# Half-partition loads copied across by ScalarE, and chunk-end rows on GpSimd, in a two-layer convolution

## The chip, the cores and the metric

The kernel runs on one core of a Trainium2 chip. A core has a matrix engine (TensorE), a vector engine (VectorE, DVE in the profile), a scalar engine (ScalarE, ACT), GpSimd (POOL), and a queue engine SP that only issues transfers here. Each engine takes its instructions in the order in which they were written, and an instruction that waits for a semaphore holds up everything behind it on that engine. The metric is the device time of one execution in microseconds (us); less is better.

## What is computed

Two layers of the same form act on a tensor `x` of 8 images, 32 channels and 252 x 252 pixels, in float32. A layer normalises in 16 groups of two channels, convolves with 5 x 5 weights under reflected borders, and adds its input:

```python
def _gn(v, G=16, eps=1e-5):
    g = v.reshape(B_, G, C_ // G, H_, W_)
    m = jnp.mean(g, axis=(2, 3, 4), keepdims=True)
    s = jnp.var(g, axis=(2, 3, 4), keepdims=True)
    return ((g - m) / jnp.sqrt(s + eps)).reshape(v.shape)

x = x + _L0_conv_ref(_gn(x), L0_conv_weight)   # 5x5, padding 2 on each side, mode='reflect'
x = x + _L1_conv_ref(_gn(x), L1_conv_weight)
```

The reference forms the convolution with Fourier transforms. The kernel forms it directly.

## The kernel before, in words

**Layout.** An image is split into its even and odd rows and its even and odd columns. Each of the four combinations of parities, with 32 channels, fills one quadrant of the 128 partitions. The 5 x 5 convolution then is a 3 x 3 one on 126 x 126 points with 128 x 128 weight matrices. In the vertical direction a transform with six points (0 to 5) makes four output rows from six input rows. Normalisation is folded into the weights, which ScalarE scales once per image and layer, and the added input is folded in as `resid`.

**Chunks and slots.** An image has 8 chunks (`NCH`) of 16 rows of such points. A chunk of the first layer (`l = 0`) is read from `x` into a buffer `xs` of 128 partitions by 16 rows by 256 columns. There are two such buffers. A chunk of the second layer (`l = 1`) reads what the first layer left in `y`. The list `order` alternates one chunk of the first layer of image b + 1 and one of the second layer of image b. I call the TensorE work for one chunk a slot.

**A table of times sets the order.** No scheduler moves anything. Each piece of work is entered in a table by `at(t, fn, ...)`; the table is sorted by `t`, and that is the order of the instructions on every engine. The times are only places in that order. `begin(i)` is the place where slot i begins; `t0` and `t1` are the beginnings of the present and the next slot.

**Loading a chunk.** `load` (L143) issues one transfer on SP's queue for each quadrant and run of rows. The partitions 0 to 63 hold the odd columns of the padded row and 64 to 127 the even ones; but every quadrant is loaded with all columns, at an offset of one column. `borders` (L148 to L154) lets GpSimd write the reflected columns, with three small copies for a chunk. Where `once(b, c)` holds, only the two quadrants of partitions 0 to 63 are loaded, and `even_columns` (L159) copies their odd positions to the even positions of partitions 64 to 127. ScalarE does so, except in one case at the start. In the kernel before, `once` holds for chunks 0 to 6 of image 0 and 0 to 2 of image 1.

**The transform of a chunk.** `transform` fills buffers that TensorE reads. VectorE makes differences of rows (`row_pairs`, L562, first layer only), two weighted differences (`row_quads`, L571 and L572, written to the buffer `u12`), the same for the rows that reach into the next chunk (`last_rows`, L578 and L579), and then the six points (L587, L591, L594, L597, L604). For the second layer the sums of rows in `v` come instead from transfers that GpSimd issues (`row_sums`, L552, then the accumulating L554 and L555). `columns` (L613 to L623) prepares points 0 and 5 where they are multiplied "by columns": fewer products, with one step more. Points 0 and 5 then also pass through the tag `u12`, which has one buffer.

**The products.** `conv` has TensorE form points 2 and 4 into `m`, points 1 and 3 into `pairs` (L680), and points 0 and 5 into `sums05` or `extra`. ScalarE seeds `pairs` from `m` (L724, L726), copies `m` (L732) and `pairs` (L739) out, and VectorE combines them (L743 to L766). By columns, `seed_columns` (L706) is a ScalarE instruction between two groups of `extra` products:

```python
        def seed_columns():
            A.activation(middle(2), middle(1), AF.Copy, scale=0.5)
...
            for i in range(4):
                at(t0 + (11.05 if i % 2 else 8.5) + 0.2 * i, column_product, 2 - i % 2, i // 2)
            at(t0 + 9.3, seed_columns)
```

Here `t0` is the slot's beginning; the first group stands at 8.5, the seed at 9.3, the second group, which adds onto the seeded sums, at 11.05. `reflect` (L864 to L867) writes the borders of `y`, `store` copies results to `o` (L917), `squares` (L855) and `piece_sums` (L231, L237) collect statistics, all on ScalarE.

## Time and profile before

| | us |
|---|---|
| Median of three runs | 1892.61 |
| Lowest and highest | 1891.02, 1893.24 |
| The profiled execution's own time | 1893.14 |
| Its span in the profile | 1891.4 |
| TensorE (PE) busy | 1851.5 |
| VectorE (DVE) busy | 1698.0 |
| ScalarE (ACT) busy | 1401.1 |
| GpSimd (POOL) busy | 372.9 |

The span runs from the first to the last recorded instruction, and the profiled execution's time is a little longer. A busy time is the time in which an engine had an instruction under way. Waits are told apart by what ended them: "PE extra L702 <- ACT extra L706" is time in which TensorE stood before the instruction of line 702 until ScalarE's instruction of line 706 was done. Lines of the order of time give start, duration, engine, source line, operation, output and input; a bracket tells how long the engine had been idle before, and what ended that.

### The profile page before, as it was taken

How to read it: one execution, taken by the hardware profiler on the slowest of the kernel's cores; microseconds unless marked ns; L12 is line 12 of the kernel's file. 1: busy time of each engine (PE TensorE's matmuls, PEld its weight loads, DVE VectorE, ACT ScalarE, POOL GpSimd, SP SyncE). 2: the span in 40 equal slices, each digit the busy share in tenths (PEclk: the TensorE clock that was granted, in tenths of full speed). 3: DMA queues.
4: the chain of work that ended last, by engine and by line, in shares of the span. 5: the costliest groups of instructions: out<-in, count | busy, mean ns of one | idle time of the engine just before them, and what ended most of it. 6: DMA issues, size and time to landing. Idle time of an engine off the chain costs nothing.

```text
span 1891.4 us, 20043 instructions
## 1 busy us (share of the span) xinstructions
PE 1851.5 (98%) x5162; PEld 956.7 (51%) x5162; DVE 1698.0 (90%) x2972; ACT 1401.1 (74%) x2695; POOL 372.9 (20%) x733
## 2 busy tenths in 40 slices
PE   5999999999999999999999999999999999999997
PEld 4444455545555555544555455555555545554455
DVE  7987899999998999999899898999989999998685
ACT  5887678778777787778787687877787765565665
POOL 4543211120112210131111310113111131111210
PEclk8999999999999999999999999999999999999999
DMA  9887899999999999999999989999999978995785
GB/s 278 205 176 191 201 248 230 212 229 253 219 239 239 206 249 233 212 244 219 246 224 229 220 214 258 221 227 226 215 260 220 236 184 177 193 203 145 192 217 113
DMA packets 248627, 411.41 MB, mean 218 GB/s; under 512 B 19520, under 2 KB 215488, under 8 KB 238144
## 3 DMA queue, kind: packets, MB, share of 16 engines
q1 hardware_dynamic: 220384, 272.09, 61.8%
q0 software_dynamic: 27648, 135.28, 28.7%
q10 hardware_dynamic: 480, 2.77, 0.4%
q8 instruction: 41, 0.67, 0.2%
q14 instruction: 74, 0.61, 0.1%
HBM read 207.41 MB, written 67.39 MB: 145 GB/s over the span
## 4 chain that ended last, share of the span: by engine, by line
PE 76%; DVE 9%; DMA 8%; ACT 3%; issue 2%; POOL 1%; SPq 0%; DVEq 0%; ACTq 0%; POOLq 0%
PE m L680 27%; PE pairs L680 26%; PE sums L680 8%; PE sums L702 6%; PE extra L702 6%; DMA v<-y 4%; PE extra L680 4%; DMA st<-in_x_dram 1%; DMA xs<-in_x_dram 1%; DMA out_dram<-o 1%; DVE sd L743 1%; ACT o L917 1%; DMA v<-ytail 1%; DVE t L604 1%; POOL u L479 0%
## 5 line engine op out<-in xcount | busy, mean ns | idle before, releaser
L680 PE MATMUL pairs<-t,u 128*128 128x504 f32 (+2 forms) x1548 | 690.4, 585 | 2.7 <-ACT pairs L726 1.6
L680 PE MATMUL m<-t,u 128*128 128x508 f32 (+3 forms) x1560 | 675.2, 581 | 7.1 <-DVE t L591 2.6
L680 PEld LDWEIGHTS m<-t,u 128*128 128x128 f32 x1560 | 293.3, 189 | 325.6 <-issue 297.4
L680 PEld LDWEIGHTS pairs<-t,u 128*128 128x128 f32 x1548 | 289.2, 189 | 321.5 <-issue 295.6
L917 ACT COPY o<-y 64x508 f32<-64x508 f32 x496 | 327.2, 660 | 8.9 <-DMA out_dram<-o 0.2
L743 DVE SCALAR_TENSOR_TENSOR sd<-sd,pairs 128x504 f32<-128x504 f32 (+2 forms) x258 | 163.9, 670 | 19.2 <-PE pairs L680 16.0
L680 PE MATMUL sums<-t,u 128*128 128x508 f32 (+5 forms) x408 | 175.3, 578 | 0.0
L855 ACT ACTIVATE junk<-y,negk 128x1008 bf16<-128x1008 f32 (+1 forms) x144 | 147.4, 1024 | 30.6 <-PE extra L702 14.9
L726 ACT COPY pairs<-m 128x504 f32<-128x504 f32 (+1 forms) x129 | 72.5, 562 | 129.6 <-PE m L680 110.0
L732 ACT COPY sd<-m 128x504 f32<-128x504 f32 (+2 forms) x258 | 137.0, 583 | 32.0 <-DVE sums L789 24.7
L604 DVE SCALAR_TENSOR_TENSOR t<-v 128x1024 f32<-128x1024 f32 (+1 forms) x128 | 157.5, 1230 | 3.5 <-PE sums L680 3.5
L702 PE MATMUL extra<-sdiff,wc 128*128 128x252 f32 (+3 forms) x616 | 156.3, 375 | 3.3 <-ACT extra L706 2.6
L702 PEld LDWEIGHTS extra<-sdiff,wc 128*128 128x128 f32 x616 | 113.5, 188 | 89.6 <-issue 50.2
L591 DVE SCALAR_TENSOR_TENSOR t<-v 128x512 f32<-128x512 f32 (+2 forms) x129 | 89.7, 695 | 65.6 <-DMA v<-y 47.7
L702 PE MATMUL sums<-d,u 128*128 128x252 f32 (+3 forms) x616 | 142.3, 373 | 0.0
L562 DVE TENSOR_TENSOR v<-xs 128x1792 f32<-128x1792 f32 (+1 forms) x65 | 129.5, 1993 | 1.8 <-issue 0.7
L554 POOL DMA_DIRECT2D v<-y x64 | 55.2, 863 | 377.7 <-DMA v<-y 377.7
L702 PEld LDWEIGHTS sums<-d,u 128*128 128x128 f32 x616 | 115.3, 189 | 26.9 <-issue 11.8
L237 ACT ACTIVATE st<-st,negk 128x1134 f32<-128x1134 f32 x98 | 121.7, 1242 | 3.2
L148 POOL COPY xs<-xs 64x32 f32<-64x32 f32 (+3 forms) x74 | 34.1, 461 | 450.2 <-DMA xs<-in_x_dram 330.7
L680 PEld LDWEIGHTS sums<-t,u 128*128 128x128 f32 x408 | 75.9, 188 | 80.1 <-issue 77.2
L231 ACT ACTIVATE st<-st 128x1134 f32<-128x1134 f32 x98 | 112.2, 1145 | 4.0 <-DMA st<-in_x_dram 2.8
(171 smaller groups left out, 2424.7 us busy)
## 6 DMA issues: line engine op xcount, KB each, us to landing
xs<-in_x_dram SPq DMA_DIRECT2D x176, 504.0 KB, 12.6
v<-y POOLq DMA_DIRECT2D x64, 1032.0 KB, 5.7
st<-in_x_dram SPq DMA_DIRECT2D x111, 567.0 KB, 6.9
out_dram<-o SPq DMA_DIRECT2D x488, 126.0 KB, 5.7
v<-y POOLq DMA_DIRECT2D x64, 903.0 KB, 9.9
u<-ud SPq DMA_DIRECT2D x15, 1152.0 KB, 5.6
xs<-in_x_dram SPq DMA_DIRECT2D x30, 441.0 KB, 6.7
xs<-in_x_dram SPq DMA_DIRECT2D x28, 472.5 KB, 11.1
```

The lines of the kernel that those rows point to most:

```text
L231: A.activation(junk, src, AF.Identity, accum_out=acc[:, 0, i : i + 1])
L237: A.activation(junk, src, AF.Square, bias=negk, accum_out=acc[:, 1, i : i + 1])
L562: V.tensor_sub(v[:, r0:r1], t[:, r0 + 2 : r1 + 2], t[:, r0:r1])
L591: stt(ts[b, l, c][0][:, 1, j0:j1], vt[:, :, 1], -2.0, vt[:, :, 2], ALU.mult, ALU.add)
L604: stt(t, got["vt"][:, :, 0:2], 4.0 if l else -4.0, got["vt"][:, :, 2:4], ALU.mult, ALU.add)
L680: T.matmul(dst, u[:, k, 2 - i, :], rhs[:, j0 + i0 : j0 + i1, i : i + wo], start=(i == 0 and not add), stop=(i == 2), skip_group_check=add,)
L702: T.matmul(dst[:, 0, use], w, rhs[:, use], start=(i == 2), stop=True, skip_group_check=(i != 2))
L726: A.copy(dst, src)
L732: A.copy(got["sd"][:, 1 + e], m24[e][:, 0:n])
L743: stt(d, d, -2.0, pairs13[e][:, 0:n], ALU.mult, ALU.add)
L855: A.activation(dst, src, AF.Square, bias=negk, scale=1.0 if i else -1.0, accum_out=acc[:, 1, at_ : at_ + 1])
L917: copy(got["o", h][halves[s], 0:m, cp::2], got["y"][halves[cp], r : r + m, :])
```

## The change

Three things change. First, `once` now holds for all chunks but the last of every image, except for chunk 2 of images 2 to 7. This makes 40 more chunks that load two quadrants and are copied across by ScalarE. They are loaded in one part, and load, borders and copy have new places in the order: load at 7.5 where it stood at 9.5, borders at 5.1 of the next slot where they stood at 9.0, the copy at 6.3. Second, `last_rows` runs on GpSimd, but for the first layer of image 0; the weighted difference, one instruction on VectorE, is two on GpSimd. Third, `last_rows` stands earlier, at 2.1 instead of 3.2 after the start of the transform, for the second layer and for the first layer from image 2 on.

```diff
     def once(b: int, c: int) -> bool:

-        return c < (NCH - 1, 3)[b] if b < 2 else False
+        return c < NCH - 1 and (b < 2 or c != 2)

     def parts(b: int, c: int):

         if once(b, c):
+            if b > 1 or (b == 1 and c > 2):
+                return ((0, ROWS),)
             return ((0, 10), (10, 6)) if (b, c) == (0, 0) else ((0, 2), (2, 14))
...
             u2, (t, nxt) = got["u"][:, 1], source()
+            eng = V if b + l == 0 else G
+            f = 4.0 if l else -4.0
+            if eng is V:
+                stt(u2[:, NT - 1], t[:, ROWS - 2], f, nxt[:, 0], ALU.mult, ALU.add)
+            else:
+                G.tensor_scalar(u2[:, NT - 1], t[:, ROWS - 2], f, None, ALU.mult)
+                G.tensor_add(u2[:, NT - 1], u2[:, NT - 1], nxt[:, 0])
             if l == 0:
-                V.tensor_sub(got["v"][:, ROWS - 2 : ROWS], nxt[:, 0:2], t[:, ROWS - 2 : ROWS])
-            stt(u2[:, NT - 1], t[:, ROWS - 2], 4.0 if l else -4.0, nxt[:, 0], ALU.mult, ALU.add)
+                eng.tensor_sub(got["v"][:, ROWS - 2 : ROWS], nxt[:, 0:2], t[:, ROWS - 2 : ROWS])
...
-            for dt, fn in ((2, row_quads), (3.2, last_rows), (3.6, point2)):
+            for dt, fn in ((2, row_quads), (3.2 if l == 0 and b < 2 else 2.1, last_rows), (3.6, point2)):
...
                 for part in parts(*inputs[k]):
-                    early = once(*inputs[k]) or nb == 0
-                    at(t0 + (14.0 if nb == 0 and part[0] == ROWS else 4.0 if early else 9.5), load, *inputs[k], *part)
-                    at(t1 + (0.2 if early else 9.0), borders, *inputs[k], *part)
-                    if once(*inputs[k]):
-                        kb, kc = inputs[k]
-                        t = 5.25 if part[0] == 0 and (kb, kc) != (1, 0) else 13.55 if kb else 8.5
-                        at(t1 + t, even_columns, *inputs[k], *part)
+                    kb, kc = inputs[k]
+                    if kb > 1 or (kb == 1 and kc > 2):
+                        at(t0 + (7.5 if once(kb, kc) else 9.5), load, kb, kc, *part)
+                        at(t1 + (5.1 if once(kb, kc) else 9.0), borders, kb, kc, *part)
+                        if once(kb, kc):
+                            at(t1 + 6.3, even_columns, kb, kc, *part)
+                    else:
...
```

In the branch left out at the end the lines of before stand unchanged.

## The prediction

> **What bounds the kernel now.** I read the page's totals first, then TensorE's waits, then one slot of the order of time on three engines. A slot is the work of one chunk on TensorE; first-layer (l = 0) and second-layer (l = 1) slots alternate.

> ```profile
> PE 1851.5 (98%) x5162; PEld 956.7 (51%) x5162; DVE 1698.0 (90%) x2972; ACT 1401.1 (74%) x2695; POOL 372.9 (20%) x733
> ...
> PE   5999999999999999999999999999999999999997
> ...
> DMA  9887899999999999999999989999999978995785
> ```

> TensorE is full from the second slice to the last, and the transfers nearly are. That busy share counts pipelined matmuls, so I read the waits too:

> ```profile
> PE m L999 <- DMA st<-in_x_dram: 15.1, 1, 15.1
> PE m L680 <- DVE t L591: 2.6, 2, 2.0
> PE extra L702 <- ACT extra L706: 2.6, 9, 0.9
> PE m L680 <- DVE var L369: 2.1, 1, 2.1
> ```

> The 15.1 us lie in the head, which the change leaves alone. All other waits that the list gives TensorE come to about 15 us, of which some 12 lie behind the head. So nothing taken from another engine can win more than some 10 us (0.5%), while a new wait ahead of a matmul costs its full length.

> One slot of l = 0 near 250 us, TensorE, then ScalarE, then VectorE (start, duration, engine, line):

> ```profile
> 252.64 3.54 PE L680 MATMUL pairs<-t,u 128*128 128x504 f32 x8
> 256.02 1.01 PE L702 MATMUL extra<-sdiff,wc 128*128 128x252 f32 x4
> 256.87 1.85 PE L680 MATMUL pairs<-t,u 128*128 128x504 f32 x4
> 258.56 1.01 PE L702 MATMUL extra<-sdiff,wc 128*128 128x252 f32 x4
> ```

> ```profile
> 253.31 1.07 ACT L732 COPY sd<-m 128x504 f32<-128x504 f32 x2
> 255.43 0.58 ACT L739 COPY sd<-pairs 128x504 f32<-128x504 f32 x1 [1.04 <-PE pairs L680]
> 255.90 0.23 ACT L864 COPY y<-y 128x16 f32<-128x16 f32 x1
> ...
> 257.07 0.57 ACT L706 ACTIVATE extra<-extra 128x504 f32<-128x504 f32 x1 [0.36 <-PE extra L702]
> ```

> ```profile
> 253.46 1.21 DVE L617 TENSOR_TENSOR d<-t 128x1008 f32<-128x1008 f32 x1
> 254.70 0.70 DVE L571 SCALAR_TENSOR_TENSOR u<-y 128x516 f32<-128x516 f32 x1
> ```

> The second group of `extra` products (258.56) needs ScalarE's seed at L706, which ends at 257.64: 0.92 us to spare. L617, the last step of `columns`, ends 3.9 us ahead of that group. Over the slots of this kind it ends between 1.6 and 3.9 us ahead; 3.9 is where VectorE has caught up with TensorE (in the even-chunk slots perhaps 0.5 more).

> [...] the copy of 64x14 elements that takes 0.20 us alone took 2.01 us at 71.59, beside VectorE's L562 (71.50 to 73.53), and near our slot a copy of 64x32, 0.23 us alone, took 1.25 us beside L617:

> ```profile
> 253.52 1.25 POOL L148 COPY xs<-xs 64x32 f32<-64x32 f32 x1 [6.70 <-DMA xs<-in_x_dram]
> ```

> [...] Here the clock stood at half after the 15.1 us wait; the 2.1 us waits left it at full.

> **The change, part by part.**

> 1. VectorE loses `last_rows` in 56 chunks of l = 0 (L578 and L579, 0.72 us from start to next start) and 64 of l = 1 (0.43): 40 + 28 = 68 us of 1698. TensorE hides VectorE's work almost wholly, so this is worth nothing by itself.

> 2. GpSimd gets 56 x 3 + 64 x 2 = 296 instructions. No row has 128-element forms. Between L479 (64 elements, 457 ns) and L459 (384 elements, about 1255 ns) lie 2.5 ns an element: an estimate of 0.6 us for 128 and 0.9 for 256. VectorE pays part of it back in blocked time (L591 took 1.50 us instead of 0.69 at 90.86, beside a 384-element L459): bounds 0 and 56 x 2.1 + 64 x 1.2 = 194 us. I take half, so VectorE's total hardly falls. What hides it is VectorE's slack of about 10%.

> 3. Forty chunks load two quadrants instead of four: 98 issues less on SP's queue, 41 MB less of 411. Before, four quadrants took about 17.7 us from first issue to the last landing and the first two 8 to 13; now two must land. The reload still waits for the last reader of its buffer, formerly L579, now GpSimd's. Gain on the path: at most the few waits that a transfer caused, near 190 us and in isolated slots. I count -4 us.

> 4. ScalarE gets 40 copies of 64x2048. L159 took 1.85 us for 1792 and 0.43 for 256, so 2.1 us each, 84 us in all. ScalarE has room for the sum (74%), but where they stand matters. In the order of the built program each stands behind the two L732 copies and ahead of L739, the four reflections (L864 to L867) and the seed L706. In 33 of the 40 the slot is one by columns, with a seed that TensorE waits for; the other 7 are in a last-chunk slot.

> 5. What the copy waits for is the heart of it. It needs `borders` (three GpSimd copies); these stand on GpSimd behind `last_rows` of the second layer; and that must wait until L617 has read the buffer in which it writes (the tag u12, one buffer). Before, ScalarE's seed depended on no GpSimd instruction, and `borders` had nobody in a hurry behind it.

> So, from the end of L617 (time 0): GpSimd's scale is blocked by L571 (0.7), takes 0.6, the add is held up by L572 and ends near 2.1; three border copies take 0.55 alone and up to 1.6 when L587 and L597 come between. I take 3.2 us; bounds 1.9 (nothing blocked) and 3.7. Hand-over to ScalarE about 0.1; copy 2.1; L739 to the end of L706 1.8 (255.43 to 257.64, less the 0.36 wait there); hand-over to TensorE 0.1. Sum 7.3 us after L617, where TensorE's second group comes 3.9 after it. It stalls 3.4 us. Behind it on TensorE's queue stand the `sums` products and the whole next slot. Where VectorE is later than 3.9 the first stall is longer, but each stall lets VectorE catch up, so 3.9 is the lasting value. It does not improve by itself: L617 hangs on the previous slot's pair products, which TensorE finishes later too.

> Sum: 33 x 3.4 = 112; seven last-chunk slots, where the copy pushes L739 and the root at L371 by about 2 us but VectorE has 2 to 4 us of room before the next products, 1 us each (bounds 0 and 3), 7; freed transfers -4. Together +115. The profiled execution had a span of 1891.4 and a time of 1893.1, near the median of 1892.6; I add to that median and round down a little, because at even chunks the freed 0.7 us of VectorE can widen the 3.9: 2004.

> **The rivals.**

> [...] If GpSimd's five instructions run in 1.9 us and the spare is 3.9 to 4.4, the stall is 1.6 to 2.1 us: 33 x 1.6 to 2.1 is 53 to 69, with the last-chunk slots 1946 to 1970. For it: some GpSimd copies in the trace run unstretched beside VectorE. Against: two stretched examples above.

> *A worse stall.* If GpSimd needs 3.7 and the landing of two quadrants (12 us after a late issue) or VectorE's lag adds another 1 us[...], each slot loses 4.5 or more: 33 x 4.5 = 149 and some 10 around it, 2050 and up.

> *Not slower: the chain is hidden.* With 68 us less on VectorE and a tenth less traffic, the waits of VectorE on the row sums (L591 on the transfer to v, 47.7 us) may vanish and VectorE run further ahead. The point from which it decides: L617 would have to end over 7.3 us ahead of the second `extra` group (6.0 if nothing is blocked) instead of 3.9. Then only the gain of part 3 is left: 1883 to 1893. Against it: in the slots where VectorE waits for nothing but TensorE, the distance is 3.8 to 3.9 again and again. That the change doesn't do what it says I exclude: in the built program VectorE has 176 instructions less, GpSimd 296 and ScalarE 40 more.

> **How the numbers follow.** The chain with a blocked GpSimd (stall 2.5 to 4 us, 1972 to 2040): 0.66. [...] Worse: 0.11. Hidden: 0.10, of which faster 0.05, same 0.03, slower 0.02. A difference of 0.2% (3.8 us) is about what a measurement of this kernel can tell from none. The range leaves out the hidden case and most of the worse one: 1946 to 2048. Slower is 0.66 + 0.13 + 0.11 + 0.02 = 0.92.

> **What would show it.** TensorE's waits would have a line for L702 on ScalarE's seed (L714 in the new numbering) near 110 us in 33 to 40 waits of about 3.4 us, instead of 2.6 us in 9. ScalarE's timeline would show the 64x2048 copy idle ahead of `borders` for 2 to 3 us. GpSimd's 128-element instructions would take over 0.6 us beside VectorE. VectorE's waits on the transfer to v would shrink, and the DMA row fall by about a tenth. I am wrong if the copy runs right behind L732 without waiting, if `extra` waits under 1 us, or if TensorE's wait appears elsewhere, at `m` or `pairs`.

## The result, and the profile after

The changed kernel took 2082.2 us (median of four runs, 2080.2 to 2086.0), beside 1892.6 for the kernel before on the same chip: a ratio of 1.1006, 95% interval 1.0987 to 1.1025. The forecast was 2004 with a range of 1946 to 2048. The direction was right; the loss of 190 us was well above the 112 forecast, and outside the range.

In the changed file the lines of `row_quads` and of what stands above it in the transform are 2 further down, and those behind `last_rows` are 8 further down: L571 is now L573, L591 is L599, L617 is L625, L680 is L688, L702 is L710, L706 is L714, L739 is L747. `last_rows` itself is at L584, L585 and L587.

The page of the changed kernel: busy time of each engine, then TensorE's and the transfers' rows in forty slices.

```profile
PE 1912.7 (92%) x5162; PEld 986.3 (47%) x5162; DVE 1706.0 (82%) x2796; ACT 1477.0 (71%) x2735; POOL 654.0 (31%) x1029
...
PE   6998989989899898998899988999889998999997
...
DMA  9768669677587675776667856777667765465785
```

TensorE runs the same 5162 instructions, now with holes in every second or third slice, and it is *busier* by 61.2 us. The span grew by 188.3 us, from 1891.4 to 2079.7: 61.2 are busy time, and 127.1 are TensorE's idle time (167.0 instead of 39.9). The transfers' row fell, with 370.13 MB moved instead of 411.41.

The waits of the changed kernel (engine, line and what it waited for, then us in total, times, longest):

```profile
POOL u L584 <- DVE d L625: 425.1, 47, 18.4
...
ACT xs L159 <- POOL xs L151: 147.4, 43, 4.8
...
PE extra L710 <- ACT extra L714: 127.5, 41, 5.9
...
DVE t L595 <- POOL u L585: 21.6, 47, 2.5
...
DVE t L599 <- DMA v<-y: 7.3, 3, 4.4
```

From the top this is the forecast chain: GpSimd's `last_rows` (L584) waits for `columns` (L625), ScalarE's copy (L159) for `borders` (L151), TensorE for the seed (L714). TensorE's wait was 2.6 us in all before and is 127.5 now, about what its idle time grew by. VectorE's wait on the transfer to `v` fell from 47.7 to 7.3.

One slot of l = 0 near 265 us, in order of time (start, duration, engine, line). VectorE ends `columns` and goes on to the next transform:

```profile
262.80 1.21 DVE L625 TENSOR_TENSOR d<-t 128x1008 f32<-128x1008 f32 x1
264.04 0.70 DVE L573 SCALAR_TENSOR_TENSOR u<-y 128x516 f32<-128x516 f32 x1
```

GpSimd can begin only then, with `last_rows` and then `borders`:

```profile
264.17 0.97 POOL L584 TENSOR_SCALAR u<-y 128x129 f32<-128x129 f32 x1 [8.30 <-DVE d L625]
265.22 0.41 POOL L585 TENSOR_TENSOR u<-u,y 128x129 f32<-128x129 f32 x1
265.58 0.23 POOL L148 COPY xs<-xs 64x32 f32<-64x32 f32 x1
265.75 0.67 POOL L150 COPY xs<-xs 64x16 f32<-64x16 f32 x1
266.37 0.73 POOL L151 COPY xs<-xs 64x16 f32<-64x16 f32 x1
```

ScalarE stands idle for 3.34 us, copies, and comes to the seed last:

```profile
267.12 2.02 ACT L159 COPY xs<-xs 64x2048 f32<-64x2048 f32 x1 [3.34 <-POOL xs L151]
269.17 0.58 ACT L747 COPY sd<-pairs 128x504 f32<-128x504 f32 x1
...
270.35 0.57 ACT L714 ACTIVATE extra<-extra 128x504 f32<-128x504 f32 x1
```

Here one sees that ScalarE takes its instructions in order: the input of L747 is ready near 264.8 (an estimate: 2.8 us after the pair products begin, as in the slot shown of the kernel before), yet L747 starts only at 269.17, behind the copy.

TensorE, for its second `extra` group:

```profile
266.27 1.85 PE L688 MATMUL pairs<-t,u 128*128 128x504 f32 x4
270.97 1.12 PE L710 MATMUL extra<-sdiff,wc 128*128 128x252 f32 x4 [2.85 <-ACT extra L714]
```

From the end of L625 (264.01): `last_rows` is done 1.6 us later, `borders` 3.1, the copy 5.1, the seed 6.9. The forecast had 2.1, 3.2, 5.4 and 7.2. Its two hand-overs of 0.1 us were 0.02 to ScalarE (267.10 to 267.12) and 0.05 to TensorE (270.92 to 270.97). TensorE's second group was due 4.1 us after L625 (forecast 3.9) and stood for 2.85.

The first by-columns slot of an image's copies is worse, and here the added busy time shows itself. TensorE near 460 us:

```profile
451.48 1.12 PE L710 MATMUL extra<-sdiff,wc 128*128 128x252 f32 x4
...
460.13 2.05 PE L710 MATMUL extra<-sdiff,wc 128*128 128x252 f32 x4 [5.84 <-ACT extra L714]
461.97 6.08 PE L688 MATMUL sums<-t,u 128*128 128x508 f32 x12
```

The group behind the stall takes 2.05 us where the like group before it took 1.12, and the twelve `sums` products 6.08 where the kernel before needed 5.27 for twelve. TensorE's clock is at half after the stall: the granted clock is 0.50 from 456.75 to 463.57 us, and was 1.00 from 447.8 to 452.0. In the records of the granted clock, half-clock stretches last 24.2 us in all before (head and end only) and 143.9 after, in 25 stretches.

How much of the 61.2 us is that? Only the time in which TensorE works at half clock costs anything, and in part of these stretches it stands idle. At half clock a product of 128x508 starts every 847 ns (median of 31 in the changed kernel), at full clock every 426. Laid over each other, the records of the clock and of the products give 107.4 us of busy time at half clock, and 5.4 before. At twice the time for a product, half of the added 102.0 is lost: 51.0 us (an estimate from these two records). The other 10.2 I put down to the breaks themselves. TensorE's records, whose ends are modelled, form 31 unbroken pieces before and 70 after, and each break costs near 0.27 us of busy time: without a wait the group took 1.01 us and its record overlapped that of the group ahead by 0.16 (258.56, where the one ahead ends at 258.72); behind a wait at full clock it takes 1.12 and overlaps nothing.

### The profile page after: what moved, and what is told of

Its sections match the earlier page's. It is cut to its first block, busy times and chain, and to the rows that moved or that the text cites. A ratio compares the mean times of both kernels' runs of the same rounds, so it can differ in the third digit from the quotient of the medians.

```text
span 2079.7 us, 20123 instructions
## 1 busy us (share of the span) xinstructions
PE 1912.7 (92%) x5162; PEld 986.3 (47%) x5162; DVE 1706.0 (82%) x2796; ACT 1477.0 (71%) x2735; POOL 654.0 (31%) x1029
## 2 busy tenths in 40 slices
DMA packets 206100, 370.13 MB, mean 178 GB/s; under 512 B 17952, under 2 KB 172960, under 8 KB 195616
## 5 line engine op out<-in xcount | busy, mean ns | idle before, releaser
L688 PE MATMUL pairs<-t,u 128*128 128x504 f32 (+2 forms) x1548 | 692.2, 586 | 6.1 <-ACT pairs L732 3.8
L688 PE MATMUL m<-t,u 128*128 128x508 f32 (+3 forms) x1560 | 680.6, 585 | 4.1 <-DVE var L371 2.1
L688 PEld LDWEIGHTS m<-t,u 128*128 128x128 f32 x1560 | 297.8, 192 | 324.9 <-issue 299.9
L688 PEld LDWEIGHTS pairs<-t,u 128*128 128x128 f32 x1548 | 290.3, 189 | 326.4 <-issue 299.3
L710 PE MATMUL extra<-sdiff,wc 128*128 128x252 f32 (+3 forms) x616 | 177.6, 414 | 129.5 <-ACT extra L714 127.5
L710 PEld LDWEIGHTS extra<-sdiff,wc 128*128 128x128 f32 x616 | 119.9, 205 | 231.6 <-ACT extra L714 173.0
L159 ACT COPY xs<-xs 64x2048 f32<-64x2048 f32 (+4 forms) x59 | 101.0, 1715 | 147.8 <-POOL xs L151 147.4
L584 POOL TENSOR_SCALAR u<-y 128x129 f32<-128x129 f32 x64 | 56.2, 879 | 431.3 <-DVE d L625 406.8
L688 PE MATMUL sums<-t,u 128*128 128x508 f32 (+5 forms) x408 | 185.7, 606 | 0.0
L554 POOL DMA_DIRECT2D v<-y x64 | 39.7, 620 | 403.6 <-DVE t L612 377.9
L710 PE MATMUL sums<-d,u 128*128 128x252 f32 (+3 forms) x616 | 158.3, 404 | 0.0
L710 PEld LDWEIGHTS sums<-d,u 128*128 128x128 f32 x616 | 127.2, 208 | 31.9 <-issue 10.6
L595 DVE TENSOR_TENSOR t<-u 128x512 f32<-128x512 f32 (+2 forms) x129 | 100.4, 778 | 35.3 <-POOL u L585 21.6
L584 POOL TENSOR_SCALAR u<-xs 128x128 f32<-128x128 f32 x56 | 65.3, 1166 | 193.3 <-ACT pairs L734 107.7
```

The lines of the kernel that those rows point to most:

```text
L159: copy(t[64:128, :, 0:256:2], t[0:64, :, 1:256:2])
L584: G.tensor_scalar(u2[:, NT - 1], t[:, ROWS - 2], f, None, ALU.mult)
L595: V.tensor_sub(ts[b, l, c][0][:, 0, j0:j1], got["u"][:, 1, j0:j1], got["u"][:, 0, j0:j1])
L688: T.matmul(dst, u[:, k, 2 - i, :], rhs[:, j0 + i0 : j0 + i1, i : i + wo], start=(i == 0 and not add), stop=(i == 2), skip_group_check=add,)
L710: T.matmul(dst[:, 0, use], w, rhs[:, use], start=(i == 2), stop=True, skip_group_check=(i != 2))
```

## The experiments

Ten kernels were run. Each edit is against the changed kernel, unless the text says otherwise.

**The copy behind the seed.** Only the place of the copy moves.

```diff
-                            at(t1 + 6.3, even_columns, kb, kc, *part)
+                            at(t1 + 9.4, even_columns, kb, kc, *part)
```

> The changed kernel with one number changed: the copy by ScalarE stands at 9.4 of the slot, behind the seed of the extra products, instead of at 6.3 ahead of it. Theory A (the loss is the chain columns, last_rows, borders, copy, seed, with the copy in front of the seed, plus the halved clock behind it): the waits of TensorE for the seed fall from 127.5 us to under 10, no clock loss in the middle, 1885 to 1900 us. Theory B (GpSimd's instructions slow VectorE[...], and TensorE then waits for VectorE): hardly a change, above 2040. Theory C (ScalarE has no room for 40 copies of 2 us wherever they stand): still above 1940, with waits for pairs or seeds elsewhere.

Measured: 1944.0 us, ratio 1.026 [1.0242, 1.0279]. TensorE's waits in this kernel:

```profile
PE pairs L688 <- ACT pairs L732: 34.8, 21, 3.2
...
PE extra L710 <- ACT extra L714: 2.2, 11, 0.2
```

The wait for the seed of L714 is gone, and 138 of the 190 us with it. But the copy still waits for `borders` (59.4 us in 37 waits), and now the next seed behind it, L732 of the pair products, is late. The expected 1885 to 1900 missed that.

**`borders` ahead of `last_rows` on GpSimd.** They stood at 5.1, just behind; now just ahead.

```diff
-                        at(t1 + (5.1 if once(kb, kc) else 9.0), borders, kb, kc, *part)
+                        at(t1 + (4.9 if once(kb, kc) else 9.0), borders, kb, kc, *part)
```

> The changed kernel with borders at 4.9 instead of 5.1, so that on GpSimd the three border copies stand ahead of the second layer's last_rows and no longer behind its wait for columns. The copy stays ahead of the seed. Theory A: the copy starts when ScalarE is free or the two quadrants have landed, so the stall falls from 3.2 us and more to between 0 and 1.5 us a slot and the clock stays up: 1895 to 1945 us. Theory B: as the changed kernel, above 2040. Theory C: above 1940.

Measured: 1998.8 us, ratio 1.0571 [1.0543, 1.06]. The waits of this kernel:

```profile
POOL xs L148 <- DMA xs<-in_x_dram: 413.7, 52, 14.6
...
PE extra L710 <- ACT extra L714: 71.1, 36, 4.4
...
DVE t L595 <- POOL u L585: 67.3, 52, 3.1
```

Freed from `last_rows`, the first border copy waits for the two quadrants to land, and `last_rows`, now behind it, is late for VectorE. So `borders` were held by two things that end near one another, and taking one away wins 83 us, not the 137 to 187 expected.

**`last_rows` back on VectorE.**

```diff
-            eng = V if b + l == 0 else G
+            eng = V
```

> The changed kernel with last_rows back on VectorE; half loads, borders and the copy ahead of the seed stay. Theory A: on GpSimd borders now wait only for the two quadrants to land, as in the run with borders first (1999 us), so the copy is still held up, by the transfer instead of by columns: 1975 to 2010 us, TensorE's waits for the seed 50 to 80 us. Theory B (GpSimd's rows slow VectorE[...]): clearly less, below 1940. A third reading, that the wait on columns was all that held up the copy: 1893 to 1925.

Measured: 1958.3 us, ratio 1.0331 [1.0303, 1.036], below the range of the first expectation (1975 to 2010) and above the two others. The waits of this kernel:

```profile
POOL xs L148 <- DMA xs<-in_x_dram: 469.1, 58, 23.5
...
ACT xs L159 <- POOL xs L151: 65.5, 36, 4.9
...
PE extra L710 <- ACT extra L714: 44.5, 28, 3.5
```

Without GpSimd in the chain the landing holds `borders` again, and TensorE still waits 44.5 us. Both legs, `last_rows` and the landing, are real; either alone costs tens of us while the copy stands ahead of the seed.

**`last_rows` on GpSimd alone.** The kernel before, with this part and its earlier place only; loads, borders and copies are as before.

```diff
+            eng = V if b + l == 0 else G
...
+                G.tensor_scalar(u2[:, NT - 1], t[:, ROWS - 2], f, None, ALU.mult)
+                G.tensor_add(u2[:, NT - 1], u2[:, NT - 1], nxt[:, 0])
...
+                eng.tensor_sub(got["v"][:, ROWS - 2 : ROWS], nxt[:, 0:2], t[:, ROWS - 2 : ROWS])
...
-            for dt, fn in ((2, row_quads), (3.2, last_rows), (3.6, point2)):
+            for dt, fn in ((2, row_quads), (3.2 if l == 0 and b < 2 else 2.1, last_rows), (3.6, point2)):
```

> The kernel before with last_rows on GpSimd and its earlier place alone; loads, borders and copies as before, so no copy by ScalarE after image 1, chunk 2. Theory A: within 10 us of before, 1888 to 1903, since nobody in a hurry stands behind GpSimd's wait. Theory B: most of the loss is here, above 2000. Theory C: as before, 1893.

Measured: 1900.1 us (20 runs, 1893.8 to 1909.3), ratio 1.0042 [1.0032, 1.0051]. The totals of its page:

```profile
PE 1852.5 (98%) x5162; PEld 956.3 (51%) x5162; DVE 1702.2 (90%) x2796; ACT 1401.0 (74%) x2695; POOL 644.9 (34%) x1029
```

VectorE has 176 instructions less, and its busy time rose from 1698.0 to 1702.2: what it saved it paid in longer instructions, in a kernel in which GpSimd has 272 us more of recorded work. No run takes apart why they are longer. TensorE is unmoved, so this part costs almost nothing without the copy behind it. The 8 us of the median aren't seen in the profiled execution, which took 1893.8, the lowest of the twenty; their cause stays open.

**The copy at the slot's end.** Only the place of the copy moves, behind all that the slot has for ScalarE.

```diff
-                            at(t1 + 6.3, even_columns, kb, kc, *part)
+                            at(begin(i + 2) - 0.05, even_columns, kb, kc, *part)
```

> The changed kernel with the copy moved to the end of the slot, behind the seed, the statistics and the squares, right ahead of the outer rows of the second layer (L776), where ScalarE waits for TensorE. Theory A (only the place of the copy on ScalarE's queue costs time): TensorE waits for nothing new, no clock loss, 1885 to 1903 us. Theory C (ScalarE has no room for 40 copies of 2 us): seeds of pairs are late as in the run with the copy behind the seed (1944 us), above 1925.

Measured: 1912.4 us, ratio 1.0096 [1.0081, 1.0112]. The waits of this kernel on ScalarE's seeds:

```profile
PE pairs L688 <- ACT pairs L732: 8.5, 20, 2.9
...
PE extra L710 <- ACT extra L714: 1.8, 8, 0.2
```

So 170 of the 190 us hang on the place of the copy. Everything else of the change is still in this kernel: GpSimd's `last_rows`, the halved loads, the 40 copies.

**The same, and `last_rows` on VectorE.** Both edits together.

```diff
-            eng = V if b + l == 0 else G
+            eng = V
...
-                            at(t1 + 6.3, even_columns, kb, kc, *part)
+                            at(begin(i + 2) - 0.05, even_columns, kb, kc, *part)
```

> The copy at the end of the slot as before, and last_rows back on VectorE: the half loads alone, with a copy nobody waits for. last_rows on GpSimd alone cost 8 us (1900 against 1892), so Theory A expects 5 to 10 us less than with the copy last and the rows on GpSimd, 1882 to 1895; if freeing VectorE helps once transfers are fewer, it is the other way round.

Measured: 1904.1 us, ratio 1.0056 [1.0041, 1.0071]: 8.3 less than the kernel with the copy at the slot's end, inside the expected step of 5 to 10, though the level was missed by 9. What remains, 11.5 us (10.7 beside runs of the kernel before on the same chip), is 40 copies on ScalarE and half the loads. TensorE waits 8.3 us for L732, of which 2.9 in one place and some 0.28 each in the others: the copy stands just ahead of that seed.

**The copy behind that seed too.** `last_rows` on VectorE, the copy 2.75 after the start of the next slot.

```diff
-            eng = V if b + l == 0 else G
+            eng = V
...
-                            at(t1 + 6.3, even_columns, kb, kc, *part)
+                            at(begin(i + 2) + 2.75, even_columns, kb, kc, *part)
```

> The kernel with the copy at the slot's end and the rows on VectorE still took about 12 us more than the kernel before, and TensorE waited 8.3 us for the pair seed of line 732, which stands just behind the copy. This kernel moves the copy behind that seed (2.75 after the start of the next slot). If the pair seed carries the rest, its line falls to about the 1 to 2 us of the kernel before and the time is 1893 to 1898. If the rest is ScalarE's greater load wherever the copy stands, 1901 to 1906. If the copy is now too late for VectorE's rows of the next chunk, a new wait of VectorE on ScalarE's copy appears and the time is above 1908.

Measured: 1919.1 us, ratio 1.0135 [1.0114, 1.0156]. The waits of this kernel on ScalarE's seeds:

```profile
PE extra L710 <- ACT extra L714: 18.5, 21, 1.3
...
PE pairs L688 <- ACT pairs L732: 2.3, 3, 1.0
```

The pair seed is on time, as expected, and the time is above 1908, but not for the reason given: VectorE waits under 2 us for the copy. The seed of L714 in the second layer's slot is late instead, up to 1.3 us. None of the four places tried makes the copy of 2 us free. No version run beats the kernel before.

**Filling the wait.** Does the halved clock cost what the records say? Fourteen products of an identity, which change no result, keep TensorE at work ahead of the waiting group in the 33 slots.

```diff
...
+        def keep_busy():
+            T.matmul(m24[1][:, 0:P], ident, ident, start=True, stop=True)
...
             at(t0 + 9.3, seed_columns)
+            if copied(b, l, c):
+                for _ in range(14):
+                    at(t0 + 11.04, keep_busy)
```

> The changed kernel, and in the 33 slots where the copy stands ahead of the seed TensorE gets 14 small products of the identity, 128 columns each, about 3 us in all, into a bank that is free there, right before the group that waits for the seed. The wait for the seed stays, only filled. If the 60 us of the loss that the wait itself does not cover are the clock[...]: the clock stays up and the time falls by 45 to 65 us to between 2017 and 2037. If the low clock has another cause[...], filling the waits leaves it at 2075 or above.

Measured: 2045.5 us, ratio 1.0807 [1.0791, 1.0823]: adding 108 us of useless work (33 groups of 3.29) made the kernel 37 us *faster*. Half-clock stretches fell from 143.9 to 38.0 us, and TensorE's busy time in them from 107.4 to 19.8, which gives back 43.8. The expected 2017 to 2037 was missed, mainly because the filling and what is left of the wait come to 139.3 us (108.4 + 30.9) where the wait alone was 127.5. From the span after, 2079.7 + 11.8 - 43.8 makes 2047.7; the profile has 2042.6, and these 5 us have no place in the sum.

**Half of the copy moved.** If the clock drops for long stalls only, stalls shorter by 1 us should leave it alone. Eight rows stay at 6.3, eight go to the slot's end; line numbers are 4 higher.

```diff
+    def half_copy(b: int, c: int, h: int):
+        r = slice(8 * h, 8 * h + 8)
+        A.copy(xs[b, c][64:128, r, 0:256:2], xs[b, c][0:64, r, 1:256:2])
...
-                            at(t1 + 6.3, even_columns, kb, kc, *part)
+                            at(t1 + 6.3, half_copy, kb, kc, 0)
+                            at(begin(i + 2) - 0.05, half_copy, kb, kc, 1)
```

> Of each of the 40 copies only the first 8 rows stay ahead of the seed; the other 8 are copied at the slot's end. Each stall ahead of the second extra group should be 1.0 us shorter: 127.5 becomes about 95. [...] Then the stalls of 2.85 to 3.85 us, now 1.8 to 2.9, leave it at full, and only the first slot of each image (5.84, now 4.8) still lowers it: half-clock stretches of 50 to 75 us in all instead of 144, TensorE busy 1868 to 1880, and the time 2005 to 2020. Rival: the clock follows TensorE's mean idle share and not the single stall. Then it loses in proportion, about 45 us instead of 61: half-clock stretches of 105 to 120 us, busy about 1897, and the time 2030 to 2045.

Measured: 2052.7 us, ratio 1.0844 [1.0822, 1.0865]. Both expectations fell. The wait shrank as it should, to 95.5 us, but half-clock stretches *rose*, to 154.9 us in 34 stretches, and TensorE's busy time to 1917.8. The stall of one and the same slot can be compared in the two kernels. TensorE's order of time in the changed kernel:

```profile
495.95 1.12 PE L710 MATMUL extra<-sdiff,wc 128*128 128x252 f32 x4 [3.25 <-ACT extra L714]
```

In this kernel:

```profile
489.82 2.05 PE L714 MATMUL extra<-sdiff,wc 128*128 128x252 f32 x4 [2.36 <-ACT extra L718]
```

After 3.25 us idle the group runs at full speed, after 2.36 at half. The length of the stall does not decide.

What does decide is in the clock records of all kernels. In the twelve profiles (before, after and these ten) every change of the clock falls on a grid of 3.413 us. I laid that grid over TensorE's busy and idle times, with one shift of 11.2 us between the clock's records and the span for all of them. The shift was chosen so that it fits, but the traces bear it out: in their own timestamps the spans begin at 10.9 to 11.3 us, and with each trace's own value the five counts are 0 of 6378, 13 of 37, 78 of 78, 0 of 91 and 22 of 22. A shift that is off by 0.3 us fits less well (72 of 79 in the third line). The head and the end are left out.

| clock in a cell of 3.41 us | TensorE idle in that cell | next cell at half clock |
|---|---|---|
| full | under 1.7 us | 0 of 6369 |
| full | 1.7 to 2.05 us | 15 of 36 |
| full | over 2.05 us | 76 of 76 |
| half | under 0.5 us | 0 of 91 |
| half | over 0.64 us | 22 of 22 |

The 3.25 us of the first line lie across two cells, 1.61 and 1.64 us in each; the 2.36 us of the second lie with 2.20 in one cell. (The last kernel, below, is counted in the table; without it the rule reads the same.)

**Splitting the wait.** The test of that reading, on the kernel with the half copies: four products, which change no result, that can start when ScalarE's copy of L747 is done, so that they cut the wait in two.

```diff
...
+        def split_wait():
+            T.matmul(m24[1][:, 0:P], ident, got["sd"][:, 0, 0:P], start=True, stop=True)
...
+            if copied(b, l, c):
+                for _ in range(4):
+                    at(t0 + 11.04, split_wait)
```

> The kernel with the half copies, and four products of 128 columns (about 0.9 us) that TensorE can start as soon as ScalarE's copy of line 747 is done, some 1.2 us before the awaited seed; they change no result. A wait of 2.4 us becomes about 1.2 idle, 0.9 busy, 0.3 idle, and ends no earlier. Reading of the clock records so far: the clock is set anew every 3.41 us, and goes to half where TensorE was idle for more than about 1.9 us of the 3.41 before. If that holds, only the first slot of each image (4.96, now some 3.7 in one piece) still halves it: half-clock stretches of 40 to 65 us in all instead of 155, TensorE's busy time falls from 1918 to 1892 to 1902 although it has 30 us more work, and the time falls from 2052.7 to 1998 to 2014. If the halving hangs on the length of the wait or on what the other engines do, the stretches stay near 155 us, busy rises to about 1948 and the time stays at 2045 to 2058.

Measured: 2030.1 us, ratio 1.073 [1.071, 1.075]. TensorE in the slot of the line shown above (L721 is the added product):

```profile
483.58 1.16 PE L721 MATMUL m<-sd,ident 128*128 128x128 f32 x8 [1.19 <-ACT sd L758]
484.76 1.12 PE L718 MATMUL extra<-sdiff,wc 128*128 128x252 f32 x4
```

The group runs at full speed again. Half-clock stretches fell from 154.9 us to 58.3, from 34 to 12, inside the expected 40 to 65: the halving hangs on idle time within a cell. The time was missed by 16 us, and TensorE's busy time, 1919.8, by 18. The four products take 1.16 us at full clock (38.2 in all, not 30), and the clock gives back 40.5 (busy time at half clock 38.3 instead of 119.3): 1917.8 + 38.2 - 40.5 makes 1915.5, and some 4 us have no place in this sum.

| kernel | us | span of the profile | TensorE idle | TensorE busy | half-clock stretches | busy at half clock |
|---|---|---|---|---|---|---|
| before | 1892.6 | 1891.4 | 39.9 | 1851.5 | 24.2 | 5.4 |
| after | 2082.2 | 2079.7 | 167.0 | 1912.7 | 143.9 | 107.4 |
| half of the copy at the slot's end | 2052.7 | 2051.8 | 134.0 | 1917.8 | 154.9 | 119.3 |
| `borders` first | 1998.8 | 1995.9 | 111.3 | 1884.6 | 69.6 | 47.0 |
| `last_rows` on VectorE | 1958.3 | 1953.8 | 82.9 | 1870.9 | 48.7 | 28.3 |
| copy behind the seed | 1944.0 | 1943.3 | 78.0 | 1865.3 | 38.7 | 19.1 |
| copy at the slot's end | 1912.4 | 1909.2 | 51.4 | 1857.8 | 28.9 | 8.4 |
| the same, rows on VectorE | 1904.1 | 1900.5 | 46.9 | 1853.6 | 21.4 | 3.6 |

Down this path the 189.6 us are 169.8 for the place of the copy (after to copy at the slot's end), 8.3 for `last_rows` on GpSimd, and 11.5 for the rest. The parts don't add in any order: with the copy left in its place, `last_rows` on VectorE alone gives back 123.9.

## Why the prediction was right and wrong

**What bounds the kernel: right.** TensorE had nothing to win. With the copy out of the way and `last_rows` on VectorE, 41 MB less traffic left the kernel 11.5 us slower than before, not faster, though it still carried the 40 copies; with `last_rows` on GpSimd, VectorE's lighter program wasn't lighter in time either. That its total "hardly falls" was right: it rose by 4.2 us in the kernel that changed this alone.

**Parts 4 and 5, the chain: right, link by link.** The slot shown has 1.6, 3.1, 5.1 and 6.9 us where the sum had 2.1, 3.2, 5.4 and 7.2. The lines named in advance appeared: the wait at L710 for the seed (127.5 us in 41 waits, 32 of them over 2 us, forecast near 110 in 33 to 40), the copy idle ahead of `borders`, the shorter wait on `v`. The moved copy shows that the chain is the cause, and not only the place where time is booked: 170 us go with it alone. Two smaller things were otherwise. In the slot shown only the scaling in `last_rows` took over the 0.6 us named (0.97; the add took 0.41); and the landing of the two quadrants, which the text put under the worse stall, is a second leg close behind the first: with `last_rows` back on VectorE, TensorE still waits 44.5 us for the seed.

**The lasting spare of 3.9 us: wrong in one slot of each of six images.** "Each stall lets VectorE catch up, so 3.9 is the lasting value" holds in most slots, whose stalls are 2.85, 3.25 and 3.85 us. In an image's first by-columns slot with a copy, the chain was 7.5 us long (L625 ended at 452.54, the seed at 460.07), 0.6 more than in the slot shown, and L625 ended only 1.7 us ahead of the due time, 454.28, so that the stall was 5.84. Six images pay this anew. It makes the mean stall 3.75 instead of 3.4: 120 us in 32 stalls where the sum had 112.

**The sum: it lacked a term of 61 us.** This is the step that failed. Each stall was priced at its own length, with TensorE's clock left at full. As measured, the 188.3 us of the span are 127.1 of idle time, where the sum had 115, and 61.2 of added busy time, where it had nothing: 51.0 for work at half clock and 10.2 for the breaks. The profile before has the clock at half in its head and at its end alone: it stood at half after the wait of 15.1 us and at full after those of 2.1, and nothing in it lies between the two. So what a stall of 3.4 us does to the clock was not shown, and leaving it at full was an estimate. The clock records of the twelve profiles show it: cells of 3.413 us on a grid that doesn't follow the stalls, and about 2 us of idle time inside one cell were enough (over 2.05 us in 76 of 76 cells). A stall of 3.4 us leaves at least 1.7 us in one of two neighbouring cells and up to all of it, so by these records most such stalls halve the clock. In the changed kernel, 20 of the 32 stalls over 2 us at L710 did. The added products and the split wait show that this term is real.

**The last-chunk slots: half the size.** 7 us were counted, 1 us for each of seven slots. The stalls came one slot later, at the seed of the second layer. The first of them, and the same place in the kernel before:

```profile
416.01 1.03 PE L710 MATMUL extra<-sdiff,wc 128*128 128x256 f32 x4 [0.74 <-ACT extra L714]
```

```profile
392.36 1.02 PE L702 MATMUL extra<-sdiff,wc 128*128 128x256 f32 x4 [0.21 <-ACT extra L706]
```

There are six, of 0.74 to 1.05 us, 5.5 us in all, beside 2.0 in the same six places before: 3.5 more. With the copy at the slot's end no wait for this seed is longer than 0.2 us, so they hang on the copy's place too. One new wait of 3.2 us, for the pair seed near 197 us, was not forecast.

**Rivals.** The rival with a stall of 1.6 to 2.1 us asked for GpSimd's five instructions in 1.9 us; they took 3.1 in the slot shown. "Hidden" asked for L625 to end 7.3 us ahead; it ended 4.1 ahead where it was earliest among the slots read closely. The rival that came true is the worse stall (2050 and up), and mostly not by a longer chain: the 3.7 us that it asked of GpSimd were 3.1 in the slot shown and the mean stall was 3.75 us, while 51.0 us are work at half clock. How much GpSimd's instructions lose to VectorE's beside them in this chain (the scaling took 0.97 us beside L573, the add 0.41) no run takes apart.

**My own expectations** for the moved copy were too low by 9 to 44 us, each time because the work moved was taken out of one queue and not priced in the place where it was put.

## What to carry to other kernels

Price a new wait on a full matrix engine with its clock: lay the stall into cells of the clock's grid, and where it can leave some 2 us idle in one, add the next cell at half speed (here over 2.05 us of idle time halved it in 76 of 76 cells, and this was 51 us beside 127 us of idle time). A long copy on an engine that also feeds small seeds to TensorE belongs behind the seed, and its whole chain (who writes its input, and what stands ahead of that on the other queue) should be walked before it is placed. Two inputs that arrive near one another must both be made early; moving one shows the other.
